# Scores and transposed scores in one visit: two sets of four PSUM banks that change places

## The chip, the cores and the metric

The kernel runs on one core of a Trainium2 chip. The core has a matrix engine (TensorE, PE in the profile), a vector engine (VectorE, DVE), an engine for activation functions (ScalarE, ACT), a general engine (GpSimd, POOL) and DMA queues. PE writes its results to PSUM, which has eight banks; here a bank holds 512 fp32 numbers in each of 128 partitions. DVE and ACT read PSUM; POOL does not. The metric is the device time of one execution in microseconds (us), lower being better.

## What is computed

The reference is one pre-norm decoder layer over 2 batches of 512 tokens of width 1024, in three parts that each add to the running x:

```python
x = x + attn(layernorm(x), w_qkv, b_qkv, w_o, b_o)          # 32 query heads, 8 key/value heads of width 32
x = x + matmul(fake_quant(layernorm(x)), fake_quant(ctx))   # 8-bit rounding of both sides
x = x + ffn(layernorm(x), W_org, lora_down, lora_up, lora_keys, Wq)
```

The first is causal attention with rotary positions. The second multiplies the rounded rows by a rounded context matrix. The third is a dense product and eight low-rank products, mixed by a softmax over keys per batch. The change concerns the first part, and what is run beside it.

## The kernel before

**The attention loop.** Queries are handled in 16 chunks of four heads (8 chunks for each batch). A head is 32 wide, so four heads occupy the four 32-row strips of the matrix array, and one head goes to each of four PSUM banks. Two chunks make five slots, 40 slots in all; `QUERIES` and `KEYS` say which blocks of 128 queries or keys share a slot, so that a slot's part of a bank is 384 or 512 columns.

A slot i does two different things:

- `scores(i)` multiplies queries by keys into the four-bank tile `sc`. DVE adds the mask, writes the negated scores to SBUF (`ms`) and keeps each row's least value; ACT takes the exponential and the row's total (`stats`). These serve only to find the normaliser of each row.
- `weights(i - LAG)`, for the slot four earlier, multiplies keys by queries (the scores transposed, `st`), adds each row's normaliser by a small bf16 matmul (`mT`), and ACT takes the exponential of all four banks in one instruction (`pt`). POOL clears the part above the diagonal.

When all scores of a chunk are known, `split` computes the normalisers (a logarithm and an exponential on ACT, two small operations on DVE, six on POOL), and `turn_terms` transposes them by a DMA that ACT issues. `attend(g)` then multiplies `pt` by the values into one bank (`pv`), and a copy puts the result into `oT`.

The eight banks are: one four-bank tile shared in turn by `sc` and `st` (pool `ps_sc`, one buffer), one bank for `pv`, and three for everything else (`ps_mm`).

**The fillers.** Between these steps PE runs other work. The projections of queries, keys and values are done as seven products per column block (a Strassen scheme); each product is a *unit* of four full matmuls into one bank, followed by one or two adds on DVE (`add`) and, where a result is complete, by four DVE operations of the rotary embedding (`rotate`). After the first batch's attention, the fillers are its output projection (`W`, eight matmuls a unit), the column sums `cs`, the context products `C` and transposes `X` (the queue entry `post`).

**What sets the order.** The order of instructions on each engine is fixed when the program is written out; on the chip each engine works through its own list and waits where it must. A planner (`Clocks`) keeps an estimate of each engine's time as it writes. `fill(us)` gives PE so many microseconds of filler, one matmul at a time, with a running `credit`. `hold(us)` adds filler while PE would otherwise wait more than 0.3 us. `dispatch` places waiting DVE and ACT steps (from `lanes`) when their engine would be free, at most 0.6 us ahead of PE. `force` and `need` place a step, or run filler, because something is due. In the old loop `fill` runs twice per slot, after `scores` and after `weights`, by `SLOT_S` and `SLOT_T`. `W_first` starts the first output tile while attention of the first batch is still being finished. When all scores are out, `last_resort` lets `hold` take matmuls from the second batch's output product (`beside`).

After the loop the tail (second batch's output product, dense product, hidden and up products) runs with eight banks in rotation.

Of the kernel before, what the change touches and what calls it, by code (L numbers as in the profile page):

```python
# [47 lines left out]
SLOT_S = (2.7, 3.2, 0.8, 2.7, 0.8)  # L48
SLOT_T = (1.8, 2.2, 2.2, 1.8, 2.2)
FILL_1 = 116.0  # L50
FILL_2 = 80.0
# [47 lines left out]
class Clocks:  # L99
# [6 lines left out]
    def __init__(self, nc):  # L106
        self.nc = nc
        self.seen = 0
        self.at = {"PE": 0.0, "DVE": 0.0, "Activation": 0.0, "Pool": 0.0, "DMA": 0.0}
        self.written = {}  # L110
        self.read = {}
        self.before = {}
        self.slots = {}
        self.used = {}
        self.tile_size = None

# [26 lines left out]
    def add(self, ins):  # L143
# [69 lines left out]
        for name, part in sources:  # L213
            self.read[name].add(part, done or end, engine)
        self.log(ins, engine, names, start)
# [6 lines left out]
def kernel(  # L222
# [58 lines left out]
    ps_mm = pool("ps_mm", 3, space=PSUM)  # L281
# [7 lines left out]
    beginning = ExitStack()  # L289
    ps_first = pool("ps_first", 5, beginning, space=PSUM)  # L290
# [66 lines left out]
    mm_pools = [ps_mm, ps_first, ps_first, ps_mm, ps_first, ps_first, ps_mm, ps_first]  # L357
    mm_count = [0]

    unread = []  # L360
    opened = [0]

    def settle(n):

        unread[:] = [key for key in unread if key not in done]
        while len(unread) > n:
            force(unread[0])
            unread[:] = [key for key in unread if key not in done]

    def mm(shape, name, dtype=F32):  # L370

        settle(2 if mm_pools[1] is ps_mm else 5)
        mm_count[0] += 1
        return mm_pools[mm_count[0] % len(mm_pools)].tile(shape, dtype, tag="mm", name=name)
# [24 lines left out]
    def transpose_f32(dst, t, src, name):  # L399

        for g in range(NK // 4):
# [5 lines left out]
            evacuate(dst[g][:, :, t * P : (t + 1) * P], ps)  # L407

# [68 lines left out]
    last_resort = [iter(())]  # L477
    weighted = [0]
    attended = [0]

# [19 lines left out]
    def may_start(key):  # L500
        if key == "post":
            return attended[0] >= NC - 1
# [24 lines left out]
    def fill(us):  # L527

        credit[0] += us
        while credit[0] > 0 and any_may():  # L530
            if not step():
                credit[0] = min(credit[0], 3.0)
                break

    def hold(us):

        while clocks.now("PE") + HOLD < us:
            if not (any_may() and step()) and next(last_resort[0], None) is None:
                break
# [99 lines left out]
    def add(col, dst, ps, other, key, bias=None, in_mm=True):  # L639
# [10 lines left out]
        if in_mm:  # L650
            unread.append(key)
# [14 lines left out]
    def g_kept(c, part=WHOLE, bank=None):  # L666
# [5 lines left out]
        if bank is None:  # L672
            unread.append(key)
# [3 lines left out]
        )  # L677

    def g_first(c, part=WHOLE, bank=None):
# [6 lines left out]
        add(c, dst[:, part], ps[:, part], place(c, 1, 0)[:, part], key, 0, bank is None)  # L686
        if last:
            complete(c, 0, 0, dst, key)

    def g_second(c):  # L690
# [7 lines left out]
        add(c, both, ps, both, ("U2", c))  # L698
        if c == COLUMNS[-1]:
# [5 lines left out]
        add(c, more, ps, both, ("U4", c))  # L705
        force(("S", 4))
# [4 lines left out]
        complete(c, 0, 1, dst, ("C12", c))  # L711

    def g_third(cols):

        for c in cols:
# [5 lines left out]
            add(c, more, ps, more, ("U7", c), 1)  # L721
            force(("T", c, 4))
# [3 lines left out]
            complete(c, 1, 0, both, ("C21", c))  # L726
        for c in cols:
# [9 lines left out]
    def g_values(b, halves_):  # L737
# [10 lines left out]
        for half, ps in zip(halves_, banks):  # L748
            evacuate(vs[b][:, :, half * P : (half + 1) * P], ps)
            if not b:  # L750
                q_live[0] -= 1

# [129 lines left out]
    banks = [mm([P, S], f"first_kv{i}") for i in range(4)]  # L882
# [16 lines left out]
    first_kv(slice(2 * P, S))  # L899

# [37 lines left out]
    settle(0)  # L938
    beginning.close()
    mm_pools[:] = [ps_mm] * 3  # L940
    ps_sc = pool("ps_sc", 1, attn, space=PSUM)
    ps_pv = pool("ps_pv", 1, attn, space=PSUM)
# [46 lines left out]
    last_sc = [None]  # L989

    def sc_free():

        clocks.catch_up()
        return clocks.read[last_sc[0].name].last() if last_sc[0] is not None else 0.0

# [3 lines left out]
    def scores(i):  # L999


        pair, j = divmod(i, NS)
        sc = ps_sc.tile([P, 4, S], F32, tag="sc", name=f"sc{i}")
        parts = []
        at_col = 0
        for n, t in QUERIES[j]:
            g = 2 * pair + n
# [3 lines left out]
            klen = (t + 1) * P  # L1011
            part = slice(at_col, at_col + klen)
            at_col += klen
            parts.append((g, t, klen, part))
            for s in range(4):
# [3 lines left out]
                    kTs[b][row(s), c // 4, :klen],  # L1019
# [3 lines left out]
        last_sc[0] = sc  # L1023
        for s in range(4):
            whole = msp.tile([P, S], F32, tag="ms", name=f"ms{i}_{s}")
            for g, t, klen, part in parts:
                ms = whole[:, part]
                least = stats[g][:, t, s, 0:1]
                nc.vector.tensor_tensor_reduce(  # L1029
                    out=ms,  # L1030
                    in0=sc[:, s, part],
                    in1=mask[:, S - klen :],
                    scale=-scale,
                    scalar=BIG,
                    op0=ALU.add,
                    op1=ALU.min,
                    accum_out=least,
                )
                nc.scalar.activation(  # L1039
                    ms,  # L1040
                    ms,
                    AF.Exp,
                    bias=least,
                    scale=-1.0,
# [1091 lines left out]
```

## Time and profile before

| | |
|---|---|
| time, median of 3 runs | 677.82 us (677.25 to 678.95) |
| span of the profiled execution | 675.4 us |
| attention loop in that execution | 45.8 to 414.1 us |
| PE busy | 647.2 us, 96% of the span |
| DVE busy | 504.2 us, 75% |
| ACT busy | 299.3 us, 44% |
| POOL busy | 93.5 us, 14% |

The span runs from the first to the last instruction of one execution; the time also holds what lies around it, here 2.4 us beside the median.

A timeline line reads: start, duration, engine, source line, operation, the tile written, the tiles read, shape, and how many instructions are merged; in brackets, idle time before it and what ended that. A line by windows reads: the stretch, its length, then busy time and number of instructions of PE, PE's weight loads, DVE, ACT and POOL, then the granted clock, the DMA share and GB/s. A line of waits reads: who waited, for whom, microseconds in total, how often, and the longest. The chain that ended last is followed back from the last instruction, at each step to whatever released it. One fp32 matmul of the program is two matmul instructions in the trace, and "a full matmul" below is one such instruction, 128 x 128 by 512.

### The profile page before, as it was taken

The page shows a single profiled execution, that of the slowest core. Times are in us where ns is not written, and L with a number is a line of the kernel's source. Part 1 is how long each engine was busy: PE and PEld are TensorE (multiplying, and loading weights), DVE is VectorE, ACT ScalarE, POOL GpSimd, SP SyncE. Part 2 cuts the span into 40 slices and gives each one's busy share as a digit, 9 for nine tenths or more (in the row PEclk, how much of TensorE's full clock was granted, in tenths as well). Part 3 has the DMA queues.
Part 4 walks back from the last instruction along what each step waited for, and adds up shares of the span by engine and source line. Part 5 has one row for each costly group of instructions (what it writes and reads, how often), then busy time and mean ns, then how long its engine had stood idle before and what let it go on. Part 6 is the DMA issues. An engine that isn't in the chain of part 4 may idle for free.

```text
span 675.4 us, 8962 instructions
## 1 busy us (share of the span) xinstructions
PE 647.2 (96%) x3197; PEld 294.5 (44%) x3204; DVE 504.2 (75%) x1205; ACT 299.3 (44%) x695; POOL 93.5 (14%) x213
## 2 busy tenths in 40 slices
PE   5999689999999999999989999999999999999997
PEld 5754233343433434334434444444445454444443
DVE  5799689976678989777678657898969944743775
ACT  2245465666776486877767731354221100110100
POOL 2100023312222122122222321000001000000000
PEclk9999899999999999999999999999999999999999
DMA  9930000010103352102100208295100003000104
GB/s 288 324 74 0 8 9 1 9 40 9 39 2 102 101 134 40 65 14 50 24 10 1 24 9 287 93 333 97 20 28 0 1 31 124 1 0 0 63 0 186
DMA packets 42476, 44.63 MB, mean 66 GB/s; under 512 B 19264, under 2 KB 32576, under 8 KB 42432
## 3 DMA queue, kind: packets, MB, share of 16 engines
q1 hardware_dynamic: 24992, 38.82, 17.3%
q10 hardware_dynamic: 17440, 5.25, 4.8%
q8 instruction: 25, 0.41, 0.3%
q14 instruction: 19, 0.16, 0.1%
HBM read 35.66 MB, written 4.19 MB: 59 GB/s over the span
## 4 chain that ended last, share of the span: by engine, by line
PE 70%; ACT 15%; DVE 12%; issue 1%; DMA 0%; POOL 0%; ACTq 0%; DVEq 0%; POOLq 0%
PE wb L1599 14%; ACT ms L1039 8%; PE pj L657 8%; PE wo L1599 7%; PE up L1682 7%; PE h L1646 7%; ACT pt L1115 7%; DVE ms L1029 5%; PE sc L1016 5%; PE st L1098 3%; PE ct L1248 3%; PE wo L1248 3%; PE first_kv L657 2%; PE pj_v L657 2%; PE pv L1141 2%; PE pj_k L657 1%
## 5 line engine op out<-in xcount | busy, mean ns | idle before, releaser
L1039 ACT ACTIVATE ms<-ms,stats 128x512 f32<-128x512 f32 (+3 forms) x256 | 140.2, 549 | 84.0 <-DVE stats L1029 81.5
L1029 DVE CUSTOM_DVE_ANT_0 ms<-sc,mask 128x512 f32<-128x512 f32 (+3 forms) x256 | 108.3, 485 | 34.8 <-PE sc L1016 31.8
L1115 ACT ACTIVATE pt<-st 128x2048 f32<-128x2048 f32 x40 | 74.8, 1870 | 38.3 <-PE st L1106 38.1
L657 PE MATMUL pj<-xT,wq 128*128 128x512 f32 x192 | 90.9, 606 | 0.0
L1118 POOL TENSOR_SCALAR_AFFINE_SELECT pt<-pt 128x512 f32<-128x512 f32 x64 | 47.4, 757 | 245.2 <-ACT pt L1115 245.2
L1098 PE MATMUL st<-qT,kT 32*128 32x128 f32 (+3 forms) x512 | 49.5, 461 | 4.9 <-DVE stats L1029 4.8
L657 PEld LDWEIGHTS pj<-xT,wq 128*128 128x128 f32 x192 | 33.8, 189 | 40.3 <-issue 39.7
L1016 PE MATMUL sc<-kT,qT 32*128 32x128 f32 (+3 forms) x512 | 45.8, 460 | 4.1 <-ACT pt L1115 1.4
L1039 ACT ACTIVATION_READ_ACCUMULATOR ms<-ms,stats 128x1 f32 x256 | 47.8, 187 | 0.0
L1248 PE MATMUL wo<-wo,oT 128*128 128x512 f32 x96 | 46.6, 613 | 0.0
L1016 PEld LDWEIGHTS sc<-kT,qT 32*128 32x128 f32 x512 | 22.4, 184 | 39.6 <-ACT pt L1115 26.5
L1141 PE MATMUL pv<-pt,v 128*32 128x128 f32 (+3 forms) x512 | 37.8, 436 | 0.0
L1098 PEld LDWEIGHTS st<-qT,kT 32*128 32x128 f32 x512 | 21.1, 185 | 32.6 <-DVE stats L1029 18.8
L1248 PE MATMUL ct<-q,q1T 128*128 128x512 bf16 x123 | 28.0, 379 | 1.3 <-DVE oT L382 0.8
L1599 PE MATMUL wb<-tb,S 128*128 128x512 f32 x64 | 28.3, 595 | 0.0
L1599 PE MATMUL wb<-worg,S 128*128 128x512 f32 x64 | 28.0, 592 | 0.0
L1599 PE MATMUL wb<-worg,x3T 128*128 128x512 f32 x64 | 27.8, 592 | 0.0
L1141 PEld LDWEIGHTS pv<-pt,v 128*32 128x32 f32 x512 | 14.9, 109 | 29.3 <-issue 20.6
L1248 PEld LDWEIGHTS wo<-wo,oT 128*128 128x128 f32 x96 | 16.7, 189 | 21.0 <-issue 20.3
L657 PE MATMUL pj_k<-xT,wk 128*128 128x512 f32 x32 | 17.2, 667 | 5.6 <-DVE qT L648 5.6
L648 DVE TENSOR_TENSOR qT<-pj,qT 128x512 f32<-128x512 f32 x28 | 18.8, 683 | 4.2 <-PE pj L657 4.2
L1189 ACT ACTIVATE raw<-raw,qp_sb,inv_s 128x1024 f32<-128x1024 f32 x8 | 9.8, 1237 | 25.3 <-DMA raw<-in_ctx_dram 24.0
(235 smaller groups left out, 1017.6 us busy)
## 6 DMA issues: line engine op xcount, KB each, us to landing
wq<-in_wqT_dram SPq DMA_DIRECT2D x8, 512.0 KB, 8.7
ctx_raw<-in_ctx_dram SPq DMA_DIRECT2D x8, 512.0 KB, 3.3
wo<-in_woT_dram SPq DMA_DIRECT2D x8, 512.0 KB, 3.3
raw<-in_ctx_dram SPq DMA_DIRECT2D x8, 512.0 KB, 5.7
worg<-in_worgT_dram SPq DMA_DIRECT2D x8, 512.0 KB, 7.1
out_dram<-x SPq DMA_DIRECT2D x16, 256.0 KB, 2.1
x<-in_x_dram SPq DMA_DIRECT2D x7, 512.0 KB, 6.0
x_raw<-in_x_dram SPq DMA_DIRECT2D x4, 512.0 KB, 7.5
```

Source lines behind the costliest of these rows:

```text
L657: nc.tensor.matmul(ps[:, part], weight[:, k, :], xs_[:, k, part], start=(k == 0), stop=(k == n - 1),)
L1016: nc.tensor.matmul(sc[:, s, part], qTs[b, c][row(s), t * P : (t + 1) * P], kTs[b][row(s), c // 4, :klen], start=True, stop=True,)
L1029: nc.vector.tensor_tensor_reduce(out=ms, in0=sc[:, s, part], in1=mask[:, S - klen :], scale=-scale, scalar=BIG, op0=ALU.add, op1=ALU.min, ...
L1039: nc.scalar.activation(ms, ms, AF.Exp, bias=least, scale=-1.0, accum_out=stats[g][:, t, s, 1:2],)
L1098: nc.tensor.matmul(sc[:, s, part], kTs[b][row(s), c // 4, kb * P : (kb + 1) * P], qTs[b, c][row(s), kb * P :], start=True, stop=False,)
L1115: nc.scalar.activation(pt, sc[:, :, :n], AF.Exp, scale=scale)
L1118: nc.gpsimd.affine_select(out=diagonal, in_=diagonal, compare_op=ALU.is_ge, fill=0.0, base=0, pattern=[[0, 4], [1, P]], channel_multiplier=-1,
L1141: nc.tensor.matmul(pv[row(s), kb * P :], vs[b][:, kb, h * HD : (h + 1) * HD], pt[:, s, part], start=(kb == 0), stop=(kb == NT - 1),)
L1248: nc.tensor.matmul(ps, l[:, t * P : (t + 1) * P], r[:, cols], start=(k == 0), stop=(k == len(terms_) - 1))
L1599: nc.tensor.matmul(ps[i], l[:, k, i * P : (i + 1) * P], r(k), start=(k == 0), stop=(k == n - 1))
L1646: nc.tensor.matmul(ps[i], r(k)[:, i * P : (i + 1) * P], l[:, k, :], start=(k == 0), stop=(k == n - 1))
L1682: nc.tensor.matmul(ps[t], l[:, k, t * P : (t + 1) * P], r(k), start=(k == 0), stop=(k == n - 1))
```

## The change

PSUM is divided into two sets of four banks, `sets`. In each slot there is now one visit. The scores of slot i go into one set (`new`), and right behind them the transposed scores of slot i - 4 into the other (`old`). The values, where there are some, go into the first bank of `new` as soon as DVE has read it, and so do the fillers that follow, until the next visit; then the sets change places. ACT's order in a visit becomes: totals of two heads, the exponential `pt`, totals of the other two.

Fillers run in whole units only: a unit that has been opened is finished before a visit starts (`close`), a new one is begun only when the credit is over half a unit, and `hold` begins one only where a wait longer than 0.3 us and half a unit is foreseen. Before a visit, the adds that still read its filler banks are placed (`empty`). The filler time of a visit is a cycle (7.5 us, later 7.1) less the visit's own work. A unit of the output projection is split into two halves of four matmuls, each with an add of its own. `W_first` and `last_resort` go, and the first batch's output projection may start once eight chunks are attended to (before, seven). A filler that is due for a chunk is forced ahead of the visit, where it was forced behind the scores.

```diff
-SLOT_S = (2.7, 3.2, 0.8, 2.7, 0.8)
-SLOT_T = (1.8, 2.2, 2.2, 1.8, 2.2)
-FILL_1 = 116.0
-FILL_2 = 80.0
+VISIT, VALUES = 2.35, 2.35
+CYCLE_1, CYCLE_2 = 7.5, 7.1
+UNIT = 3.44
...
-    ps_mm = pool("ps_mm", 3, space=PSUM)
+    psum = pool("psum", 1, space=PSUM)
...
+    sets = [psum.tile([P, 4, 512], F32, tag=f"banks{i}", name=f"banks{i}") for i in range(2)]
...
     def mm(shape, name, dtype=F32):
 
-        settle(2 if mm_pools[1] is ps_mm else 5)
-        mm_count[0] += 1
-        return mm_pools[mm_count[0] % len(mm_pools)].tile(shape, dtype, tag="mm", name=name)
+        clocks.catch_up()
+        could = [p for p in allowed if is_free(p)]
+        if not could:
+            waiting = [p for p in allowed if reader[p] is not OPEN]
+            force(reader[waiting[0]])
+            could = waiting[:1]
+        place = min(could, key=last_read)
+        allowed.remove(place)
+        allowed.append(place)
+        ps = take_bank(place)
...
     def fill(us):
 
         credit[0] += us
-        while credit[0] > 0 and any_may():
+        while any_may() and (is_open() or credit[0] > UNIT / 2):
             if not step():
-                credit[0] = min(credit[0], 3.0)
+                credit[0] = min(credit[0], UNIT)
                 break
 
+    def close():
+
+        while is_open():
+            step()
+
     def hold(us):
 
-        while clocks.now("PE") + HOLD < us:
-            if not (any_may() and step()) and next(last_resort[0], None) is None:
-                break
+        while clocks.now("PE") + HOLD + UNIT / 2 < us and any_may() and step():
+            close()
...
-            return attended[0] >= NC - 1
+            return attended[0] >= NC
...
+    def visit(i):
+
+        pair, j = divmod(i, NS)
+        old, new = filler[0], 1 - filler[0]
+        g = 2 * pair + j // 2 - 3 if j in (2, 4) else -1
+        if i < n_slots and j in (0, 2):
+            begin_chunk(2 * pair + j // 2)
         if j in (0, 3) and i + 2 < n_slots:
             ahead = made_by(2 * pair + (1 if j == 0 else 2))
             while ahead and ahead not in done:
                 step()
+        if g >= 0:
+            values_of(g)
+        close()
+        when_free = [last_read((new, s)) for s in range(4)]
         if i >= LAG:
+            of = {n for n, _, _ in turned(i - LAG)}
+            for n in sorted(of):
+                force(("mT", n))
+            when_free += [when([mT[n]]) for n in of]
+        hold(max(when_free))
+        empty([(old, s) for s in range(4)])
+        of = {}
+        sc, st = sets[new], sets[old]
+        if i < n_slots:
+            scores(i, sc)
+        if i >= LAG:
+            weights(i - LAG, st)
+        for s in range(4):
+            if s == 1 and g >= 0:
+                pv = take_bank((new, 0))
+                attend(g, pv)
+            if s == 2 and i >= LAG:
+                terms_of(i - LAG, st)
+            if i < n_slots:
+                least_of(i, sc, s, of)
+                total_of(i, s, of)
+        if g >= 0:
+            attended_to(g, pv)
+        filler[0] = new
+        allowed[:] = [(new, s) for s in range(4)]
         dispatch()
+        fill((CYCLE_1 if i <= n_slots // 2 + LAG else CYCLE_2) - VISIT - VALUES * (g >= 0))
         if i < n_slots and j in (2, 4):
             g = 2 * pair + j // 2 - 1
             split(g)
...
+    for i in range(n_slots + LAG):
+        visit(i)
+    close()
+    empty(every)
...
     run_some(4)
-    attend(last - 1)
+    pv = mm([P, S], "pv")
+    attend(last - 1, pv)
+    attended_to(last - 1, pv)
     run_some(5)
```

## The prediction

> **What bounds the kernel now.** I read the page first, then busy time by stretch, then TensorE's own timeline, then the waits.
>
> ```profile
> span 675.4 us, 8962 instructions
> ...
> PE 647.2 (96%) x3197; PEld 294.5 (44%) x3204; DVE 504.2 (75%) x1205; ACT 299.3 (44%) x695; POOL 93.5 (14%) x213
> ...
> PE 70%; ACT 15%; DVE 12%; issue 1%; DMA 0%; POOL 0%; ACTq 0%; DVEq 0%; POOLq 0%
> ```
>
> TensorE (PE) is nearly always busy, and the chain that ended last is mostly PE. But 30% of it runs through ScalarE (ACT) and VectorE (DVE), nearly all before 414 us, where attention ends. Busy time by stretch of the attention loop (slots 0-8, 9-19, 20-23, 24-29, 30-34, 35-38, then the end):
>
> ```profile
> 45.80:121.80 76.00, 66.80 (x341) 27.21 (x340) 65.46 (x185) 43.12 (x125) 11.36 (x27) 0.98 0.03 6
> 121.80:216.70 94.90, 93.82 (x633) 39.03 (x633) 71.59 (x216) 64.02 (x166) 21.72 (x46) 1.00 0.10 29
> 216.70:256.00 39.30, 38.55 (x228) 16.72 (x228) 34.60 (x93) 25.43 (x60) 7.40 (x20) 1.00 0.45 127
> 256.00:304.20 48.20, 47.18 (x342) 19.42 (x342) 37.39 (x119) 37.44 (x96) 11.62 (x26) 1.00 0.13 32
> 304.20:344.60 40.40, 38.78 (x279) 16.37 (x280) 25.51 (x88) 31.30 (x79) 10.12 (x24) 1.00 0.14 30
> 344.60:376.60 32.00, 30.42 (x219) 12.96 (x220) 26.45 (x80) 22.65 (x56) 8.73 (x23) 1.00 0.04 9
> 376.60:414.10 37.50, 35.80 (x287) 16.93 (x290) 20.82 (x47) 16.22 (x28) 9.89 (x19) 1.00 0.28 60
> ```
>
> After span and PE come DVE (fourth figure) and ACT. Busy PE is partly modelled, so I take its real work from start times:
>
> ```profile
> 65.07 1.14 PE L1016 MATMUL sc<-kT,qT 32*128 32x512 f32 x8
> 66.14 1.98 PE L657 MATMUL pj_k<-oT,t 128*128 128x512 f32 x4
> 70.10 3.70 PE L657 MATMUL pj_k<-xT,wk 128*128 128x512 f32 x8 [1.97 <-DVE qT L648]
> 73.73 1.15 PE L1016 MATMUL sc<-kT,qT 32*128 32x384 f32 x16
> 78.56 4.40 PE L657 MATMUL pj_k<-xT,wk 128*128 128x512 f32 x6 [3.68 <-DVE qT L648]
> ...
> 268.52 0.93 PE L1098 MATMUL st<-qT,kT 32*128 32x384 f32 x8
> ...
> 269.82 1.98 PE L1734 MATMUL wo<-wo,oT 128*128 128x512 f32 x4
> 271.87 1.15 PE L1016 MATMUL sc<-kT,qT 32*128 32x384 f32 x16
> ...
> 281.78 2.36 PE L1141 MATMUL pv<-pt,v 128*32 128x512 f32 x32
> 284.07 1.14 PE L1098 MATMUL st<-qT,kT 32*128 32x512 f32 x8
> ```
>
> Scores take 1.07 us to the next start (65.07 to 66.14), transposed scores 1.30 (268.52 to 269.82), values 2.29 (281.78 to 284.07). A full matmul takes 0.4295: the chain has 72 in 30.90 us. So the loop, 45.8 to 414.1, holds 418 full matmuls (179.5 us), 40 scores (42.8), 40 transposed scores (52.0), 16 values (36.6), 75 bf16 matmuls of 0.21 (15.9) and 36 transposes of 0.11 (4.0): 331 us of work in 368. **The other 37 us are all that the change can touch.** By stretch they are 14.1 (slots 0-8), 8.0 (9-23), 11.2 (24-38) and 3.7 (end). After 414 PE goes on at 0.43 us per matmul, and a filler matmul not done in the loop costs the same there.
>
> Of the 37, about 15.2 are array switches: eight filler matmuls from 264.89 to 268.52 took 3.63 us, not 3.44, so 0.19 each, twice a slot, 40 slots. The other 21.8 are waits, 10.7 of them in slots 0-8 (14.1 less 18 x 0.19), behind DVE.
>
> ```profile
> PEld sc L1016 <- ACT pt L1115: 26.5, 29, 1.2
> ...
> PEld st L1098 <- DVE stats L1029: 18.8, 26, 1.8
> ...
> DVE ratio L1059 <- ACT ratio L1057: 14.2, 7, 3.5
> ```
>
> These are where one four-bank tile passes from use to use. Scores wait for the exponentials (pt), transposed scores for DVE. The two weight-load waits alone are 45 us, more than PE lost to everything, so fillers already cover much of them.
>
> **The change, part by part.** I sum against the span, 675.4 us; the median, 677.8, is 2.4 above it for what lies around, which stays.
>
> *One visit per slot.* 40 switches go: -7.6. Entering the scores direct from the last filler stays. Scores to transposed scores, both 32 rows, has no row here; pv to st (281.78 to 284.07) shows nothing lost. Between 0 and 0.19 I take 0.
>
> *The floor by one set goes.* A tight slot was 183.66 to 191.39, 7.7 us: 1.35 to DVE's first read, 2.8 of reads, 1.3 st, 1.9 pt and latencies. With two sets scores wait only for the previous visit's pt. ACT's new order is two totals, pt, two totals: first total at 2.1 us into the visit, 0.98 a head (0.72 where the part is 512 wide), so pt ends at 5.5 to 6.1. With values it must wait until PE has read the old pt buffer (2.37 + 2.29 = 4.66), so it ends at 6.6 and the totals at 8.6. The visits planned (7.5 and 7.1) are longer. A mean gain of 7.7 - 6.3 in latency is worth nothing while PE is full; it pays only in waits.
>
> *Slots 0-8.* I went through them with these durations. The two waits of 1.97 and 3.68 go: they are adds queued behind score reads that waited for PE, while three projection banks were full; now adds are forced ahead of a visit. New: in visits without transposed scores the first unit goes into the bank being read, and waits about 1 us for DVE's first read (four visits, +4); and an add of the last unit is put behind the split's ratio (L1059), which waits for ACT: 2.3 in visit 5, 0.7 in visit 8. I come to visit 9 at 118.7, not 121.8, with half a unit (1.7) more done: 14.1 becomes 9.3.
>
> *Slots 9-23.* 15 switches 2.9; one more such ratio wait 0.7; the last unit's add (0.61 to 0.69, read about 0.25 after PE ends) has 1.07 of scores as cover, but DVE is busy 71.59 of 94.90 and may be one 0.7 operation behind: 0 to 0.9, taken as 0.25 a visit (nearest the lower end, since the planner lets DVE run 0.6 ahead at most), 3.75. The chunk deadlines force 34 units before visit 23, while the credit up to there (118.45 - 16.45 = 102 us) pays for 29.7: they run early in blocks, visit 23 has no filler, and PE waits for its pt, some 2.5. Sum 9.8, against 8.0.
>
> *Slots 24-38.* Credit is then negative, and an extra unit is begun only if a wait over 0.3 + 1.72 us is foreseen. A visit with values ends on PE at 4.7, its pt at 6.6: 1.9, not filled. Visits 24, 27, 29: 5.7 (0 if the planner sees a tenth more). Switches 2.9, adds 3.75, and ACT's other work (L1170 at 1.23, L1300 at 1.05) before pt, 0 to 10, taken as 4: a filled visit of 6.0 us has no slack. W's adds stand ahead of the split, so no ratio wait. Sum 16.4, against 11.2. Halving each W unit adds 8 DVE adds, 4.9 us of DVE, hidden beside PE; uncovered, 0.6 each.
>
> *The end.* The last-resort product no longer fills the drained visits; it goes to both sides of the last values (3.4 + 3.4) and covers the 0.81 us wait before 410.61. But less filler is done by then, so the last W tile ends later; from its add (385.20) to its ct was 25 us, some 13 of it a real chain, and 13.5 us of filler remain. 0 to 8, taken as 2 beside switches and pt waits of 3.5: 5.5, against 3.7.
>
> *Moved, at no cost.* The pv copy (0.69) now follows the four score reads on DVE; a filler unit of 3.44 covers it, and uncovered it delays one add by 0.69. POOL's masks (0.76 each, one or two after pt) end by 8.1, before the next visit's values want them near 8.4 to 9; late, they would hold PE by the difference. The term transposes on ACT's queue (L1074) stay behind the next visit's totals and land in 2.4 us, about 1 us before transposed scores want them; a later one stalls PE by as much. SP's loads are not moved. The first W tile starts one chunk later, after values 7.
>
> Sum: 9.3 + 9.8 + 16.4 + 5.5 = 41.0 for 37.0: **+4.0, 681.8 us**.
>
> A rule against the change: the Trainium skill's Perfetto Trace Analysis, section Matmuls, wants independent groups rotated through banks, so that evacuation overlaps the next group. Whole sets break this for a visit's last unit; by the rule alone each of 40 adds would show, 40 x 0.69 = 28 us, where the 1.07 us row of scores leaves me 0.25.
>
> **Rivals.**
> 1. *Faster: PE never waits.* Where: slots 0-8 and the value visits. If the first-read waits vanish (-4), extra units fill 24, 27, 29 (-5.7), and adds stay under scores (-9), 41 becomes about 22: 663. For it: DVE is idle for 10.5 of the 76 us of slots 0-8, and the 7.7 us floor of a slot goes. Against: fillers already covered most. It decides once waits besides switches fall below 37 - 7.6 = 29.4 us, 0.73 a slot; I have 33.4.
> 2. *DVE becomes the bound.* Every visit's transposed scores wait one more operation of 0.69, less the 0.25 counted: +18, 700. For: 65.46 busy in 76 us at the start, ropes and sums queued in order. Against: score reads start 0.61 apart though each lasts 0.685 + 0.08, so busy DVE is overstated by 0.15 a read.
> 3. *Nothing gained or lost*: waits change place within 2 us: 678.
>
> **How the numbers follow.** Forecast (slower by 0.3 to 2%) 0.36, rival 1 0.32, rival 2 0.17, rival 3 0.15. A measurement can tell 0.3% (2 us). So faster 0.32, same 0.15, slower 0.53. Low end: rival 1 at 663 less little, 662; high end: rival 2 plus a badly exposed end, 702. The likeliest case alone: 680 to 691.
>
> **What would show it.** Right: scores followed at once by transposed scores, 2.37 us together, 40 times; idle PE before transposed scores with DVE adds or L1059 as releaser; about 1 us of idle PE in the first visits; visit 9 near 119 us; PE idle near 2 us after values around visits 24 to 29. Wrong: the loop ends well before 414 with the same fillers done (rival 1), or DVE over 90% busy with PE waiting in most visits (rival 2). I would be most wrong if the planner's own clocks place units otherwise than my credits say.

## The result, and the profile after

The changed kernel takes 940.36 us (median of 4 runs, 937.92 to 941.07), the kernel before beside it 677.54 us: a ratio of 1.386, 95% interval 1.384 to 1.389. I had forecast 681.8 us. "Slower" was right, but not for my reasons, and the size was not: it lost 263 us, and I had seen 4 of them.

The page of the changed kernel:

```profile
span 938.8 us, 9013 instructions
...
PE 719.0 (77%) x3204; PEld 318.3 (34%) x3204; DVE 513.0 (55%) x1210; ACT 302.8 (32%) x698; POOL 94.7 (10%) x213
...
PE   5777878777877768767777783996678978979766
...
PEclk9998899889999998978778995999798989989988
```

PE, 96% busy before, is now busy in 77% of the span. No other engine has taken over: DVE and ACT are busy for 513.0 and 302.8 us, where it was 504.2 and 299.3, in a longer span. So this is time in which engines wait for each other. The first visit of the loop shows for what (PE and DVE of the changed kernel, in order of time; a filler unit is eight of these matmul rows, x8):

```profile
57.62 1.14 PE L1073 MATMUL banks<-kT,qT 32*128 32x512 f32 x8
...
58.94 0.69 DVE L1085 CUSTOM_DVE_ANT_0 ms<-banks,mask 128x512 f32<-128x512 f32 x1 [0.45 <-PE banks L1073]
59.56 0.08 DVE L1085 DVE_READ_ACCUMULATOR2_ANT stats<- 128x1 f32 x1
59.56 0.69 DVE L1085 CUSTOM_DVE_ANT_0 ms<-banks,mask 128x512 f32<-128x512 f32 x1
...
60.17 0.69 DVE L1085 CUSTOM_DVE_ANT_0 ms<-banks,mask 128x512 f32<-128x512 f32 x1
...
60.78 0.69 DVE L1085 CUSTOM_DVE_ANT_0 ms<-banks,mask 128x512 f32<-128x512 f32 x1
61.39 0.08 DVE L1085 DVE_READ_ACCUMULATOR2_ANT stats<- 128x1 f32 x1
...
61.53 0.70 PE L709 MATMUL banks<-xT,wq 128*128 128x512 f32 x1 [2.77 <-DVE stats L1085]
```

The filler unit at 61.53 goes into bank 0. DVE had finished with bank 0 at 59.64. PE waited until 61.47, when DVE had read bank 3, and started 1.9 us later than its own bank needed. It looks as if the wait is for the *tile* of four banks, not for the bank; the experiments below test that. It also works the other way, and then twice in a row. Here is a visit with values, first PE, then DVE (two reads a bank):

```profile
135.31 2.36 PE L1198 MATMUL banks<-pt,v 128*32 128x512 f32 x32
140.66 5.40 PE L709 MATMUL banks<-oT,t 128*128 128x512 f32 x8 [2.99 <-DVE oT L429]
```
```profile
137.85 0.42 DVE L1085 CUSTOM_DVE_ANT_0 ms<-banks,mask 128x256 f32<-128x256 f32 x1 [2.59 <-PE banks L1198]
...
139.92 0.69 DVE L429 COPY oT<-banks 128x512 f32<-128x512 f32 x1
```

The values are written to bank 0. DVE's reads of banks 1 to 3, whose scores had long been there, wait 2.59 us until the values are complete. Then PE waits 2.99 us until these reads and the copy of the values are over. The waits of PE in the loop, by what ended them (columns: total, times, longest):

```profile
PE banks L709 <- DVE stats L1085: 29.1, 15, 3.1
PE banks L1073 <- ACT pt L1173: 22.0, 7, 3.7
PE banks L709 <- DVE oT L429: 20.9, 7, 3.0
PE banks L1314 <- DVE stats L1085: 10.3, 7, 2.0
PE banks L709 <- DVE qT L701: 7.0, 9, 0.8
```

The second line is scores that go into the tile whose exponential ACT has yet to finish. The last line is the smallest form: inside a block of two units, the second (another bank) waits up to 0.8 us for the add that reads the first. Behind the loop, where eight separate banks used to rotate, the same makes PE and DVE take turns:

```profile
757.43 7.13 PE L1665 MATMUL banks<-tb,S 128*128 128x512 f32 x16 [2.48 <-DVE x L1686]
...
765.74 2.47 DVE L1686 TENSOR_TENSOR x<-x,banks 128x512 f32<-128x512 f32 x4
768.27 9.73 PE L1665 MATMUL banks<-tb,S 128*128 128x512 f32 x16 [3.71 <-DVE x L1686]
```

By stretch (ahead of the loop, loop, behind it; to set like against like, the loop here ends in both kernels with the last values, which is 410.0 us in the kernel before, where 414.1 was used above), first the changed kernel, then the kernel before; length, then busy PE, and the granted clock after POOL's column:

```profile
0.00:57.62 57.62, 41.19 (x197) 27.49 (x197) 35.67 (x81) 12.74 (x24) 7.42 (x21) 1.00 0.67 201
57.62:550.80 493.18, 375.24 (x2269) 159.95 (x2268) 278.28 (x811) 237.84 (x603) 80.51 (x182) 0.90 0.09 24
550.80:938.80 388.00, 302.53 (x740) 130.84 (x740) 199.06 (x318) 52.25 (x71) 6.72 (x10) 0.91 0.17 55
```
```profile
0.00:45.80 45.80, 38.52 (x196) 28.45 (x196) 34.41 (x80) 12.76 (x25) 7.42 (x21) 1.00 0.86 253
45.80:410.00 364.20, 347.91 (x2305) 146.93 (x2309) 277.79 (x820) 240.17 (x608) 80.83 (x183) 1.00 0.14 34
410.00:675.40 265.40, 260.80 (x697) 119.09 (x699) 192.02 (x307) 46.38 (x62) 5.30 (x9) 1.00 0.24 79
```

The start lost 11.8 us, the loop 129.0, the end 122.6. I had left the start and the end at nothing. Of the end's part some 9 us are fillers that the loop now leaves over (16 full matmuls and 24 transposes fewer by the last values, four bf16 matmuls more). The clock column shows a second price: the granted clock is 0.90 in the loop where it was 1.00, and PE's busy time is 72 us longer for the same matmuls.

**Theory T:** a write into any bank of a multi-bank tile waits for the last earlier read of *every* bank of it, and a read for the last earlier write. Making eight banks two tiles is what costs, not the order of work. **Rival V:** banks are waited for one by one, and the single visit, the whole units and what they delay are what costs.

### The profile page after: what moved, and what is told of

Read it like the earlier page. It is cut to its first block, busy times and chain, and to the rows that moved or that the text cites. A ratio compares the mean times of both kernels' runs of the same rounds, so it can differ in the third digit from the quotient of the medians.

```text
span 938.8 us, 9013 instructions
## 1 busy us (share of the span) xinstructions
PE 719.0 (77%) x3204; PEld 318.3 (34%) x3204; DVE 513.0 (55%) x1210; ACT 302.8 (32%) x698; POOL 94.7 (10%) x213
## 3 DMA queue, kind: packets, MB, share of 16 engines
q1 hardware_dynamic: 24992, 38.82, 12.3%
## 5 line engine op out<-in xcount | busy, mean ns | idle before, releaser
L1085 DVE CUSTOM_DVE_ANT_0 ms<-banks,mask 128x512 f32<-128x512 f32 (+3 forms) x256 | 109.5, 487 | 56.2 <-PE banks L1198 37.8
L709 PE MATMUL banks<-xT,wq 128*128 128x512 f32 x192 | 100.0, 662 | 39.4 <-DVE stats L1085 16.4
L1314 PE MATMUL banks<-wo,oT 128*128 128x512 f32 x128 | 66.5, 667 | 16.7 <-DVE stats L1085 10.3
L1173 ACT ACTIVATE pt<-banks 128x2048 f32<-128x2048 f32 x40 | 74.2, 1856 | 15.4 <-PE banks L1160 12.1
L709 PEld LDWEIGHTS banks<-xT,wq 128*128 128x128 f32 x192 | 37.5, 208 | 89.1 <-issue 37.5
L1073 PE MATMUL banks<-kT,qT 32*128 32x128 f32 (+3 forms) x512 | 50.9, 502 | 22.0 <-ACT pt L1173 22.0
L1314 PE MATMUL banks<-q,q1T 128*128 128x512 bf16 x128 | 36.3, 439 | 29.3 <-DMA q1T<-a_b 13.2
L1152 PE MATMUL banks<-qT,kT 32*128 32x128 f32 (+3 forms) x512 | 52.2, 485 | 7.1 <-DVE oT L429 2.9
L1100 ACT ACTIVATION_READ_ACCUMULATOR ms<-ms,stats 128x1 f32 x256 | 48.1, 188 | 0.0
L1198 PE MATMUL banks<-pt,v 128*32 128x128 f32 (+3 forms) x512 | 37.8, 435 | 0.0
L1665 PE MATMUL banks<-worg,S 128*128 128x512 f32 x64 | 32.9, 676 | 3.9 <-DVE morewb L1602 2.8
L1152 PEld LDWEIGHTS banks<-qT,kT 32*128 32x128 f32 x512 | 25.5, 212 | 26.6 <-issue 10.7
```

Of the source, the lines that this page charges most:

```text
L709: nc.tensor.matmul(ps[:, part], weight[:, k, :], xs_[:, k, part], start=(k == 0), stop=(k == n - 1),)
L1073: nc.tensor.matmul(sc[:, s, part], qTs[b, c][row(s), t * P : (t + 1) * P], kTs[b][row(s), c // 4, : (t + 1) * P], start=True, stop=True,)
L1085: nc.vector.tensor_tensor_reduce(out=of[s][:, part], in0=sc[:, s, part], in1=mask[:, S - (t + 1) * P :], scale=-scale, scalar=BIG, op0=ALU ...
L1100: nc.scalar.activation(ms, ms, AF.Exp, bias=stats[g][:, t, s, 0:1], scale=-1.0, accum_out=stats[g][:, t, s, 1:2],)
L1152: nc.tensor.matmul(sc[:, s, part], kTs[b][row(s), c // 4, kb * P : (kb + 1) * P], qTs[b, c][row(s), kb * P :], start=True, stop=False,)
L1173: nc.scalar.activation(pt, sc[:, :, :n], AF.Exp, scale=scale)
```

## Experiments

### The same order, other tiles

The first run keeps the changed order of work and makes each bank a tile. The exponential read four banks in one instruction; it is now four.

```diff
-    sets = [psum.tile([P, 4, 512], F32, tag=f"banks{i}", name=f"banks{i}") for i in range(2)]
+    G, PIECE = 1, 1
...
+    def lay_out(pool_, prefix, per):
+        home.clear()
+        for n in range(2):
+            for j in range(4 // per):
+                t = pool_.tile([P, per, 512], F32, tag=f"{prefix}{n}_{j}", name=f"{prefix}{n}_{j}")
...
+    lay_out(psum, "banks", G)
...
-        nc.scalar.activation(pt, sc[:, :, :n], AF.Exp, scale=scale)
+        for k in range(0, 4, PIECE):
+            t, at = home[sc, k]
+            nc.scalar.activation(
+                pt[:, k : k + PIECE, :], t[:, at : at + PIECE, :n], AF.Exp, scale=scale
+            )
```

> The changed kernel with the same order of work, but each of its eight banks a tile of its own; the exponential of a visit's transposed scores, which read four banks in one instruction, is four instructions of one bank each. Theory T (a write into any bank of a four-bank tile waits for the last read of every bank of it): the waits of 2 to 3 us of the first unit after a visit and of 0.7 us inside and behind units go, in the loop and behind it, and the time falls from 940 to about what I forecast bank by bank, 680 to 705; four exponentials cost ScalarE about 40 x 3 x 0.2 = 24 us beside other work. Rival V (one visit a slot and whole units are themselves what costs, the bank is waited for in any case): the same waits stay, over 850. The first unit after a visit waits about 1 us under T, about 3 us under V; the granted clock is back near 1.0 under T.

Measured: 692.17 us (691.71 to 692.3), ratio to the kernel before 1.021 (1.019 to 1.022). 248 of the 263 us are gone. In this kernel, PE's first visit with the end of DVE's first read, and PE's first visit with values:

```profile
46.15 1.14 PE L1083 MATMUL banks<-kT,qT 32*128 32x512 f32 x8
...
48.25 0.08 DVE L1095 DVE_READ_ACCUMULATOR2_ANT stats<- 128x1 f32 x1
...
48.38 3.70 PE L719 MATMUL banks<-xT,wq 128*128 128x512 f32 x8 [1.09 <-DVE stats L1095]
...
104.90 2.36 PE L1212 MATMUL banks<-pt,v 128*32 128x512 f32 x32
107.19 3.70 PE L719 MATMUL banks<-oT,t 128*128 128x512 f32 x8
```

PE goes on 0.05 us after the first read. The wait is 1.09 us where it was 2.77, and behind the values there is none. By stretch:

```profile
0.00:46.15 46.15, 38.61 (x196) 28.80 (x196) 34.50 (x80) 12.08 (x24) 7.42 (x21) 1.00 0.84 251
46.15:414.21 368.06, 339.85 (x2254) 158.91 (x2253) 274.41 (x813) 243.18 (x724) 81.41 (x181) 0.98 0.12 32
414.21:690.40 276.19, 272.30 (x760) 125.82 (x756) 197.55 (x318) 50.81 (x70) 6.40 (x11) 1.00 0.24 76
```

Against the four-bank kernel this is 11.5 us less ahead of the loop, 125.1 in it and 111.8 behind it. PE idle (span less busy) falls from 219.8 to 39.6 us; the other 68 us are busy time, and by a rough estimate the clock accounts for most of that: 650.8 busy us at a mean clock of 0.988 would be 709 at the 0.907 of the changed kernel.

Two banks to a tile, and two exponentials (`G, PIECE = 2, 2`):

> The changed kernel with tiles of two banks, two of them a set, and the exponential in two instructions. Theory T: the waits get shorter but stay: the first unit may start once two of the four reads are done, some 1.5 us after the visit instead of 2.8, and every second group behind the loop still waits. 740 to 840, between the one-bank and the four-bank kernel. Rival V: as the four-bank kernel, 920 to 945. If it comes out at the one-bank kernel's time, the wait is not by tile but by something that needs more than two banks.

Measured: 840.9 us (833.02 to 841.38), just above T's range. The longest waits are less (2.8 us for `pt`, 1.7 for `stats`), but the wait behind values is the old one: 20.9 us, 7 times, up to 3.0.

A control, since the one-bank kernel differs in the exponential too: four-bank tiles, four exponentials (`G, PIECE = 4, 1`).

> The control of the one-bank kernel: the changed kernel with its four-bank tiles, and the exponential in four instructions. Under theory T the tiles alone cost what separates this run from the one-bank kernel: 940 to 965. If four instructions were themselves what made the one-bank kernel fast, by letting the banks go one by one, this run would be near 692.

Measured: 910.01 us (two runs), 30 below the lower end of what I expected, but 218 above the one-bank kernel. The long wait is still there:

```profile
PE banks L719 <- DVE stats L1095: 28.4, 15, 3.1
```

This pair is the cleanest test of the changed order: in the two traces DVE, ACT and POOL each work through the same instructions in the same order, and only the declaration of the banks differs. So 218 us are the tiles' and four exponentials are not what makes the one-bank kernel fast; of the 248 us above, 30 go with the exponential. They are won behind the loop, which is itself 4 us longer than with one exponential: the first context product waited 13.2 us for the load of `q1T` in the changed kernel, and this run has no such wait. What else came out otherwise behind the loop I did not follow up.

### The tile alone, in the kernel before

The most direct test uses none of the changed order: the kernel before, with the five extra banks of its end as slices of one tile.

```diff
-    ps_tail = pool("ps_tail", 5, space=PSUM)
+    tail_banks = pool("ps_tail", 1, space=PSUM).tile(
+        [P, 5, 512], F32, tag="tail", name="tail_banks"
+    )
...
+    ps_tail = Joined()
```

`Joined.tile` hands out the slices `tail_banks[:, 0]` to `tail_banks[:, 4]` in turn.

> The kernel before, with one edit: behind the attention loop the five banks that were tiles of their own are slices of one five-bank tile, in the same rotation with the three others. Nothing else changes: no visits, no sets, no other order. Theory T: two groups that stand next to each other in the joined tile (two of eight in the rotation) now wait for each other's evacuation of about 0.7 us and its latency, and others where the group between them is short; the end, 261 us long, gets 30 to 90 us longer: 710 to 770. Rival V: slices of a tile are waited for one by one, 677 to 680.

Measured: 747.19 us (744.79 to 749.89), ratio 1.102 (1.099 to 1.105). The loop is untouched and the end is 70 us longer, 49 of them idle PE; the two stretches, and the first of PE's waits:

```profile
45.50:409.80 364.30, 348.50 (x2309) 147.15 (x2309) 277.89 (x820) 240.18 (x608) 80.94 (x183) 1.00 0.13 34
409.80:745.50 335.70, 282.38 (x700) 123.14 (x699) 192.88 (x307) 46.54 (x62) 5.31 (x9) 0.95 0.18 62
```
```profile
PE tail_banks L1682 <- DVE x L1691: 11.9, 4, 6.1
PE tail_banks L1599 <- DVE x L1620: 10.1, 4, 4.7
```

These waits end with DVE's adds out of the joined tile, and the kernel before has none of them. Rival V (677 to 680) falls here: nothing but the form of a declaration was changed, and the order of instructions in the two traces is the same.

### Four-bank tiles in the loop alone

```diff
+    G, PIECE = 4, 4
...
+    ps_first = pool("ps_first", 1, beginning, space=PSUM)
+    lay_out(ps_first, "first", 1)
...
+    beginning.close()
+    psum = pool("psum", 1, attn, space=PSUM)
+    lay_out(psum, "banks", G)
...
-    run_some(4)
     pv = mm([P, S], "pv")
...
-    run_some(5)
     attn.close()
...
+    ps_tail = pool("ps_tail", 1, space=PSUM)
+    lay_out(ps_tail, "tail", 1)
+    run_some(9)
```

> The changed kernel with the two four-bank tiles in the attention loop alone; ahead of it and behind it the eight banks are tiles of their own, and the product that ran in part beside the last values runs whole behind the loop. Theory T: the 11.8 us that the start lost and the 124 us that the end lost come back, the loop's 125 stay: about 940 - 136 = 804, range 790 to 820. Rival V (what is late in the loop makes the end late, or the end is slow through the lower clock alone): 900 to 935.

Measured: 841.91 us (836.29 to 844.03), 38 more than T expected. The start came back (the loop begins at 48.1 us), the loop kept its length (491.1 us), as expected. The end is 302.8 us, not 264: of the 26.6 us above the one-bank kernel's, 19.0 are two waits, both absent there:

```profile
PE tail L1334 <- DMA q1T<-a_b: 12.3, 1, 12.3
PE tail L463 <- DVE xn_c L455: 6.7, 2, 5.1
```

So part of what I had booked on the end's banks is not theirs. The wait for `q1T` stands in each of the four kernels of the changed order with one or two exponentials a slot (12.3 to 14.4 us), and in none of the six with three or four, whatever their tiles. It goes with the order that the planner wrote for that number of exponentials.

### Does the order of work help where tiles do not hold it up?

The kernel before has one four-bank tile itself (`sc` and `st`). If T holds, it pays there too. Control first, then the tile taken apart:

```diff
-        sc = ps_sc.tile([P, 4, S], F32, tag="sc", name=f"st{i}")
+        sc, tiles_ = four(f"st{i}")
...
-        nc.scalar.activation(pt, sc[:, :, :n], AF.Exp, scale=scale)
+        for k in range(0, 4, PIECE):
+            t, at = tiles_[k // PER], k % PER
+            nc.scalar.activation(
+                pt[:, k : k + PIECE, :], t[:, at : at + PIECE, :n], AF.Exp, scale=scale
+            )
```

`four` makes 4 / `PER` tiles of `PER` banks each. One tile, four exponentials (`PER, PIECE = 4, 1`):

> The control of the three others: the kernel before with its four-bank tile, and the exponential as four instructions of one bank each. The three more instructions of some 0.2 us each cost ScalarE 0.6 us a slot, 24 us in all, and delay the next scores in the slots where they wait for the exponential: 678 to 690 under both theories.

Four tiles, four exponentials (`1, 1`):

> The kernel before, with its one four-bank tile of scores made four tiles of one bank, and the exponential of the transposed scores as four instructions of one bank; the order of the work is unchanged, since the planner still counts on the last of the four reads. Theory T (tile-wide waits are in the kernel before too, in its one four-bank tile): transposed scores now wait for the first read alone instead of the fourth, so the 4.8 us that TensorE lost to that go, and some of the wait of scores for the exponentials: 670 to 677. Rival V (bank by bank already): nothing is gained and four instructions for one cost ScalarE: 678 to 685, as the run with the joined tile and four instructions.

Two and two (`2, 2`):

> As the first of these, with two tiles of two banks and two exponentials. Theory T: transposed scores wait for the second read instead of the fourth, ScalarE pays for one instruction more a slot instead of three: 671 to 677. Rival V: as before, 677 to 680.

Four tiles, and the planner counts on the first read (`last_sc[:1]` in `sc_free`):

> As the run before it, and the planner counts on the first of the four reads: transposed scores and the next scores are issued as soon as bank 0 is read, with less filler forced ahead of them. Theory T: slots may be shorter by up to two reads, 2.1 us, where fillers were forced; but the fillers are work to be done anyway, so the gain is bounded by the 21.8 us of waits in the loop: 665 to 677. Rival: the later banks are now waited for in the middle of the transposed scores, 0.6 us apiece, and it comes out slower than the run planned on the last read, 677 to 685.

| tiles x banks, exponentials a slot | median us | ratio to before (95%) |
|---|---|---|
| 1 x 4, 1 (before) | 679.50 | 1 |
| 1 x 4, 4 | 708.04 | 1.043 (1.040 to 1.046) |
| 4 x 1, 4 | 701.90 | 1.034 (1.032 to 1.037) |
| 2 x 2, 2 | 700.05 | 1.031 (1.028 to 1.033) |
| 4 x 1, 4, planned on the first read | 719.67 | 1.059 (1.057 to 1.062) |

All my ranges were too low. Splitting the exponential costs this kernel 28.5 us, far more than the 12 at most that I had allowed, and that hides T's gain unless the control is taken: apart, the tile is 6.1 us better than joined (the planner also wrote a slightly other order for it). The wait ahead of the transposed scores for `stats`, which heads the list in the control, is gone:

```profile
PE st L1106 <- DVE stats L1037: 16.6, 22, 4.6
```

Most of that wait has only moved inside the groups of transposed scores, which now wait bank by bank and count as busy meanwhile: PE's rows that write `st` take 68.09 us in all with the tile apart and 55.91 in the control. 16.6 less 12.2 leaves 4.4 us, and the loop is 4.8 us shorter.

Why splitting costs so much is not settled. ACT itself pays little: its pieces last 591 ns each but overlap, and its busy time in `pt` rises from 74.8 to 81.7 us. Of the 31.1 us by which the two profiled executions differ, 10.8 appear in the loop and the rest behind it, where waits of 9.0 us for the context's adds and 6.1 for `xn_c` are new; so a part is the order that the planner wrote with these durations. Planning on the first read was slower by 17.8 us. Its rival had the sign, but the price falls elsewhere than it said: PE's rows of the *next scores*, whose weight loads now wait for the exponentials 65 times for 25, take 67.82 us for 45.91, the transposed scores 64.23 for 68.09.

At equal tiles and equal exponentials (one-bank tiles, four exponentials) the changed order, 692.17 us and 1.021 of the kernel before (1.019 to 1.022), is faster than the old one, 701.90 us and 1.034 (1.032 to 1.037). So with four exponentials it is not the order of work that makes a kernel slow. Whether that holds with one exponential is not shown: no run has the changed order with one exponential and short waits.

### Fewer exponentials, short waits

In these three the start and the end have one-bank tiles and the loop's sets are made of tiles of different sizes (`SIZES`: 1, 3 banks; 1, 1, 1, 1; or 1, 1, 2), an exponential for each tile; the planner then counts on the last read of a tile:

```diff
+    SIZES = (1, 3)
...
-    last_read = lambda place: clocks.read[sets[place[0]].name].latest(_part(bank(place)))
+    last_read = lambda place: clocks.read[home[place][0].name].last()
```

> The same with one-bank tiles in the loop too and four exponentials: against the kernel with one-bank tiles throughout (692.2) it shows what the edge between the loop's banks and the others costs, and the product that runs whole behind the loop instead of on both sides of the last values: 693 to 702. Against the run with one and three banks it shows what two more exponentials a slot cost: 5 to 15 if ScalarE's path is what holds the visits, 0 if it is hidden.

> The changed kernel with one-bank tiles ahead of the loop and behind it, and in the loop sets of one tile of one bank and one of three, which filler units take in turn; the exponential is two instructions, over one bank and over three. It asks whether the changed order of work, with waits that are short and two exponentials instead of four, beats the kernel before. Theory T: the first unit waits for one read only, a second for reads long done, so the waits are those of the one-bank kernel; ScalarE gets back about half of what four exponentials cost it in the kernel before (28 us of time at most): 676 to 694. Rival V2 (any joined banks bring back the long waits): 720 or more.

> The same with tiles of one, one and two banks and three exponentials a slot. If the cost is in the number of exponentials it lies between the two others; if it is in the joined banks it lies below both, since two free one-bank tiles are enough for the units of a slot. 678 to 698.

Measured: 698.3 us with (1, 1, 1, 1), 723.68 with (1, 3), 694.95 with (1, 1, 2). Changing banks at the loop's ends, with the product that now runs whole behind the loop, costs some 6 us against the 692.17 of one-bank tiles throughout, in the range expected. (1, 1, 2) and (1, 1, 1, 1) have overlapping intervals (1.021 to 1.027 and 1.026 to 1.032), so one exponential less is worth little here; (1, 1, 2) lies below both others, where I had put it if joined banks were the cost, but not clearly. (1, 3) missed theory T's 676 to 694 and lies where rival V2 had it, at 720 or more, but not for V2's reason: in its loop no wait of PE is longer than 2.6 us, those for `stats` no longer than 1.4, and the loop ends 5.3 us later than with (1, 1, 1, 1). Behind it stand the two waits of the run with four-bank tiles in the loop alone (12.4 us for the load of `q1T`, 6.7 for `xn_c`). It says nothing clean about exponentials.

### The last ten microseconds

In the one-bank kernel five visits of the loop's second half follow values with no filler between. A filler unit in every visit from 25 on:

```diff
-        fill((CYCLE_1 if i <= n_slots // 2 + LAG else CYCLE_2) - VISIT - VALUES * (g >= 0))
+        if i <= n_slots // 2 + LAG:
+            fill(CYCLE_1 - VISIT - VALUES * (g >= 0))
+        else:
+            credit[0] = 0.0
+            fill(UNIT)
```

> The kernel with one-bank tiles throughout (692.2), and in the loop's second half a filler unit in every visit, those with values too, instead of two units in some and none in others. Theory: the 10 us by which that kernel stands above my forecast of 681.8 lie in the five visits that follow values at once; each loses some 0.5 us to the exponentials, 1.4 inside the transposed scores and 1.2 to the first read, 3 in all, 15 together. With a unit between, most of it goes: 676 to 686. Rival: the visits without filler wait for work that has to be done in any case (VectorE's reads, ScalarE's totals), and the stall only moves to the other visits: 689 to 695.

> The same on the kernel with tiles of one, one and two banks in the loop and three exponentials (695.0): 679 to 689 under the theory, 692 to 698 under the rival. If either run is below 677 the changed order of work, with tiles that don't hold each other up, beats the kernel before.

Measured: 687.18 us (683.58 to 689.1) with one-bank tiles, 5.0 less than without, and 694.95 with (1, 1, 2), the same as without. The first is a microsecond above the theory's range, the second is the rival's. The wait for `stats` ahead of the output projection (5.9 us, 5 times) is gone from both, and only the first became faster. So the missing filler was worth half of the ten microseconds in one kernel and nothing in the other; the rest was not found here. No version tried beats the kernel before: the best stands at 1.012 (1.007 to 1.016) of it.

## Why the prediction was wrong

**The step that failed** is the one on which all others stood: that a bank is waited for by itself. I wrote that the first unit "goes into the bank being read, and waits about 1 us for DVE's first read"; it waits for the fourth, 2.77 us. I had the last unit's add "read about 0.25 after PE ends" and covered by scores; between two units of one set it shows in full, up to 0.8. I let the values run while DVE reads the other banks; each of the two stops the other, 2.6 and 3.0 us. And I took the start and the end as untouched, though the diff turns their banks into slices of two tiles: the kernel before with such slices in its end loses 70 us. What the runs showed in its place: with the same order of instructions on DVE, ACT and POOL, four-bank tiles take 910.01 us and one-bank tiles 692.17. That 692.2 is inside my range of 662 to 702, and is the case that I had worked out but for its four exponentials; the forecast was for the other.

**The trace of before had a sign of it.** The tight slot from which I took my durations (before, PE and DVE):

```profile
183.66 1.15 PE L1016 MATMUL sc<-kT,qT 32*128 32x384 f32 x16
...
184.88 0.56 DVE L1029 CUSTOM_DVE_ANT_0 ms<-sc,mask 128x384 f32<-128x384 f32 x1 [0.51 <-PE sc L1016]
...
187.64 0.08 DVE L1029 DVE_READ_ACCUMULATOR2_ANT stats<- 128x1 f32 x1
...
187.77 0.71 PE L1098 MATMUL st<-qT,kT 32*128 32x256 f32 x8 [0.19 <-DVE stats L1029]
```

Bank 0 was read by 185.65. The transposed scores, which begin with bank 0, start at 187.77, 0.05 us after the *last* read. Here one use of a tile hands its buffer to the next, so the row hints at the rule and does not prove it; but the planner of the kernel before counts the same way (`sc_free` takes the last read of the whole tile). I added up 1.35 + 2.8 + 1.3 for this slot (the first is 1.22 in these rows), a sum that is only right if all four reads are waited for, and then costed the change as if one were. None of my rivals varied that assumption, so none came near 940.

**The finer steps**, read on the one-bank kernel, whose four exponentials the forecast did not have (its loop holds 14 us less filler; overhead is length less work, by the durations of the prediction):

| stretch | before | forecast | one-bank kernel |
|---|---|---|---|
| slots 0-8 | 14.1 | 9.3 | 11.4 |
| slots 9-23 | 8.0 | 9.8 | 7.6 |
| slots 24-38 | 11.2 | 16.4 | 26.1 |
| end of loop | 3.7 | 5.5 | 5.0 |
| sum | 37.0 | 41.0 | 50.1 |

- *One visit.* Right: scores to transposed scores cost nothing. In most visits they follow after 0.96 or 0.97 us, where I had counted 1.07.
- *Slots 0-8.* The mechanism was right: four waits for the first read, 1.09, 0.96, 1.17 and 1.43, 4.65 against the 4 counted; the add that I had hold PE for 2.3 in visit 5 holds it for 1.99. Visit 9 starts at 121.05, not 118.7; the changed kernel is at 158.3 there.
- *Slots 9-23.* 2.2 less than forecast, most of it the wait for `pt` at their end (0.69 where I had 2.5). The adds cost what I had counted, but otherwise spread: four waits of 0.4 to 1.9, 4.1 in all, for 0.25 in each of 15 visits.
- *Slots 24-38.* The mis-sized term. The visit after 23 has no filler either, and there PE waits 6.31 for queries, where I had 1.9 for `pt`. DVE's rows of the one-bank kernel say why:

```profile
261.49 0.18 DVE L1130 TENSOR_TENSOR ratio<-ratio,stats 128x16 f32<-128x16 f32 x1 [2.97 <-POOL stats L1129]
261.70 0.17 DVE L1131 TENSOR_SCALAR ratio<-ratio 128x16 f32<-128x16 f32 x1
261.79 0.74 DVE L641 SCALAR_TENSOR_TENSOR sh_q<-sh_q,bsw_sb,trig 128x512 f32<-128x512 f32 x1
262.45 0.74 DVE L644 SCALAR_TENSOR_TENSOR qT<-qT,bqk_sb,trig 128x512 f32<-128x512 f32 x1
263.23 0.69 DVE L647 TENSOR_TENSOR qT<-qT,sh_q 128x512 f32<-128x512 f32 x1
```

  The rotary operations of the next chunk stand behind the split's ratio, which waits for POOL. I had named that queue for adds, in visits 5 and 8, and not for this. The visits that follow values at once (after 27, 29, 32, 34 and 37) do stay without filler, as forecast for 27 and 29; in each the next unit then waits 1.1 to 1.3 for the first read, 5.9 in all, which I had counted for the start of the loop alone. The granted clock in this stretch of 126.9 us is 0.95; by estimate that adds up to 6 us (0.05 of it).
- *The end.* A filler not done in the loop costs the same behind it: 276.2 us from 414.21 on, against 261.3 from 414.1 on before, for 13.9 us of filler left over (9 full matmuls, 35 in bf16, 24 transposes). That holds where the end's banks are separate tiles.

**The rule that I weighed.** The Trainium skill, Perfetto Trace Analysis, section Matmuls, has independent groups rotated through banks so that evacuation overlaps the next group. I took from it 28 us, and set 0.25 a visit against it from the row of scores. The runs side with the rule, and with more than the price that I put on it: banks that rotate inside one tile hold each other up (747.19 for 677.92 with one edit in the end). This case adds that the banks have to be separate tiles for it.

## What to carry to other kernels

Before an edit gathers PSUM banks into one tile, look in the trace for a place where two engines use different banks of one tile, and see whether the second starts after the first bank or after the last; if it is the last, price every pair of write and read in that tile one after the other, in every stage that uses it. One wide read of several banks and free rotation of these banks are then alternatives: count what the split of the read costs (28.5 us in the kernel before) against what the joined tile costs (218 in the changed one). And let at least one rival vary the assumption on which all terms rest, not only the terms.

## What the runs showed that was not expected

The granted clock fell behind waits of a few microseconds and less, on a single core. After a wait of 2.96 us (changed kernel, 83.20 us), eight matmuls took 5.40 us for 3.70:

```profile
83.20:84.20 1.00, 1.00 (x2) 0.48 (x3) 1.00 (x2) 1.00 (x5) 0.00 (x0) 0.91 0.00 0
84.20:85.20 1.00, 1.00 (x3) 0.41 (x2) 0.96 (x4) 0.97 (x6) 0.12 (x1) 0.50 0.00 0
85.20:86.20 1.00, 1.00 (x3) 0.48 (x2) 0.86 (x3) 0.06 (x1) 0.66 (x1) 0.50 0.00 0
...
87.20:88.20 1.00, 1.00 (x3) 0.19 (x1) 0.00 (x0) 0.00 (x0) 0.76 (x3) 0.88 0.00 0
```

The clock was at 0.50 for about 3.4 us and fell about 0.8 us after PE had resumed work. After the wait of 2.77 us at 61.53 it did not fall at all, while shorter ones were enough elsewhere: 1.67 us before 113.80 (clock 0.50 from 114.8 to 118.1), and in the one-bank kernel 1.12 us before 369.93 (0.50 from 370.6 to 373.8). The Trainium skill, TensorE: Matmul & The Clock Gate, Part 1, describes such a gate: by it an idle window of about 3.4 us, one of a row that runs on regardless of the program, halves the clock until a busy one has passed. The half clock and its length agree with the rows. The waits that brought it on, 1.12 to 2.96 us, were shorter than such a window, and PE worked both before and behind them; here the measurement decides. So a wait of 3 us can cost 1.7 us more than itself.
